# Down products of every second expert as seven block products

## The chip, the cores and the metric

The kernel runs on one NeuronCore of a Trainium2 chip. The time is the device time of one execution in microseconds, and the median of several executions is compared. All times of single stages come from one profiled execution.

## The reference

An attention layer over a small context is added to x, and then a mixture-of-experts layer, which is what matters here (cut, with T = 2048 tokens, D = 512, I = 256, 32 experts, 8 of them per token):

```python
comb = zeros((T, E)).at[rows, tidx].set(tw)      # weight of each token's 8 experts
g = einsum('td,eid->tei', x, w1)                 # up products
u = einsum('td,eid->tei', x, w3)
a = silu(g) * u
routed = einsum('tei,edi,te->td', a, w2, comb)   # down products, weighted
sh = silu(x @ shared_w1.T) * (x @ shared_w3.T) @ shared_w2.T
out = x + routed + sh
```

Everything is fp32.

## The kernel before

**Stages.** Attention, the gate and the routing come first (to about 183 us of the profiled span), with the shared expert's products as filler. From about 211 us the 32 experts are worked through, one place k after the other. The experts are ordered by how many tokens they have, and each place has a fixed width (`CAPS`, `ORDER`) and a fixed room for tokens (`ROOM`); `begins[k]` is where place k begins in a row of 138 slices of 128 token places. A slice can be shared by two neighbouring experts.

**Tokens.** `gather` (L1451) fetches the normalized rows of one slice from DRAM into a ring `xgs` of `NG_BUF` = 8 buffers, on GpSimd's queue. `transpose` (L1492) turns them in 32x32 blocks on VectorE, an instruction of L1501 picks the slice's weights into `wt`, and copies (L1489, nearly all on ScalarE) put the blocks in place as `x_of[k % 3]`.

**Up products.** For all experts but the first and the last, `seven(k)` does both up products as a 2x2 block product with seven block products (Strassen). `weight_sums` (L1556) and `token_sums` (L1585) form its operands on VectorE, `product` (L1594) is the matmul, and `add` (L1604), a bank copy (L1647), Silu (L1629) and a multiply (L1632) put the results together in `acts_of[k % 3]`. With h half of the room, an expert with more than 512 token places of room goes in two passes of seven steps, each step two matmuls of h columns; the others go in one pass of seven steps of four matmuls. The PSUM banks come from `ps_p`, a pool of six.

**Down products.** `down(j)` (L1735) does one slice j: two matmuls (the two halves of I, one after the other into the same bank) of 512 columns, or more, narrower ones where a slice is shared. Its bank comes from `ps_y` or `ps_z` in turn, one bank each. `evict` (L1751) scales by the token's weight on ScalarE into a buffer `yw` (4 of them), and `send` (L1707) adds the rows to the output in DRAM by an indirect DMA on GpSimd's queue; an expert's scatters follow those of the place before. After the last slice of an expert, `load_weights` brings the down weights of the expert three places on, on SyncE's queue.

**The order.** It is written out by hand: each engine works through its list in the order in which the program emits it. The main loop goes over pieces (two per expert) and their steps. In a step the next up product is emitted, then what is due from earlier steps (`soon(f, after)` puts a function on the list of a later step, `tick` emits them), then some of the VectorE and ScalarE side work, and then the down products planned for this step. An expert's down products so stand among the up products of the next:

```python
many = max(len(ready_downs) - KEPT, 0)
many = many if odd else -(-many // 2)
planned = [(2 * i + 1) * steps // (2 * many) for i in range(many)]
dues = [1.0 + 1.5 * planned.count(step) for step in range(steps)]
```

`sup` and `sdn` hold the shared expert's weights and are not used once its products are done, apart from a branch `rest()` that is taken only when an expert has more tokens than its room.

Of the kernel before, what the change touches and what calls it, by code (L numbers as in the profile page):

```python
# [9 lines left out]
F32 = mybir.dt.float32  # L10
F16 = mybir.dt.float16
I32 = mybir.dt.int32
AF = mybir.ActivationFunctionType
ALU = mybir.AluOpType
# [4 lines left out]
P = 128  # L19
# [8 lines left out]
NW = 3  # L28
# [18 lines left out]
def tile_xattn_moe(  # L47
# [22 lines left out]
    TB = 512  # L70
# [862 lines left out]
    def rest():  # L933


        with ExitStack() as ctx:
            keep = ctx.enter_context(tc.tile_pool(name="keep", bufs=1))
            for b in range(B):
                xs[b] = keep.tile([P, D], F32, name=f"xr{b}")
            wp = ctx.enter_context(tc.tile_pool(name="wp", bufs=2))  # L940
            comb = keep.tile([P, NT, E], F32, name="comb")
            nc.sync.dma_start(comb, rows.rearrange("(t p) d -> p t d", p=P)[:, :, D:])

            full = [P, NT, E]
            past = keep.tile(full, F32, name="past")
            nc.vector.tensor_tensor(
                past, logits, limit.unsqueeze(1).to_broadcast(full), ALU.is_ge
            )
            nc.vector.scalar_tensor_tensor(
                past, logits, float(-BIG // 2), past, ALU.is_lt, ALU.mult  # L950
            )
            nc.vector.tensor_tensor(comb, comb, past, ALU.mult)
            with tc.tile_pool(name="ps_tr", bufs=2, space=PSUM) as ps_tr:
                for b in range(B):
                    nc.sync.dma_start(xs[b], out[b])
                    xn2[b] = xnp.tile([P, D], F32, tag="xn2", name="xn2", bufs=4)
                    nc.sync.dma_start(xn2[b], rows[ts(b, P), 0:D])
                    gate_turn(b, ps_tr.tile([P, ND, P], F32, tag="tr", name="tr"))

            def expert_sum(up, dn, e=None):  # L960

                for k in range(NTB):
                    a = wp.tile([P, NI, TB], F32, tag="a", name="a")
                    for i in range(NI):
                        gu = [ps_gu.tile([P, TB], F32, tag="gu", name="gu") for _ in range(2)]
                        for w in range(2):
                            for d in range(ND):
                                nc.tensor.matmul(
                                    gu[w],
                                    lhsT=up[:, w, d, ts(i, P)],  # L970
                                    rhs=xnT[k][:, d, :],
                                    start=(d == 0),
                                    stop=(d == ND - 1),
                                )
                        sl = wp.tile([P, TB], F32, tag="sl", name="sl")
                        nc.scalar.activation(sl, gu[0], AF.Silu)
                        nc.vector.tensor_tensor(a[:, i, :], sl, gu[1], ALU.mult)
                    for b in range(4 * k, 4 * k + 4):
                        y = ps_y.tile([P, D], F32, tag="y", name="y")
                        for i in range(NI):  # L980
                            nc.tensor.matmul(
                                y,
                                lhsT=a[:, i, ts(b % 4, P)],
                                rhs=dn[:, i, :],
                                start=(i == 0),
                                stop=(i == NI - 1),
                            )
                        if e is None:
                            nc.vector.tensor_tensor(xs[b], y, xs[b], ALU.add)
                        else:  # L990
                            nc.vector.scalar_tensor_tensor(
                                xs[b], y, comb[:, b, e : e + 1], xs[b], ALU.mult, ALU.add
                            )

            flag = nc.values_load(
                not_small[0:1, 0:1],
                min_val=0,
                max_val=1,
                skip_runtime_bounds_check_because="a flag",
            )  # L1000
            with tc.If(flag > 0):
                attention_general()
                all_weights(comb)
                with ExitStack() as ph:
                    ps_gu = ph.enter_context(tc.tile_pool(name="ps_gu", bufs=4, space=PSUM))
                    ps_y = ph.enter_context(tc.tile_pool(name="ps_y", bufs=2, space=PSUM))
                    expert_sum(sup, sdn)
            with ExitStack() as ph:
                ps_gu = ph.enter_context(tc.tile_pool(name="ps_gu", bufs=4, space=PSUM))
                ps_y = ph.enter_context(tc.tile_pool(name="ps_y", bufs=2, space=PSUM))  # L1010
                for e in range(E):
                    up = wp.tile([P, 2, ND, I], F32, tag="up", name="up")
                    dn = wp.tile([P, NI, D], F32, tag="dn", name="dn")
                    for dst, of in ((up[:, 0], w1), (up[:, 1], w3), (dn, w2)):
                        nc.sync.dma_start(dst, of[e])
                    expert_sum(up, dn, e)
            for b in range(B):
                nc.sync.dma_start(out[b], xs[b])
# [35 lines left out]
    def experts(ups, in_order, later, products):  # L1054
# [7 lines left out]
        wup = [wp.tile([P, 2, ND, I], F32, name=f"wup{r}") for r in range(NW)]  # L1062
        wdn = [wp.tile([P, NI, D], F32, name=f"wdn{r}") for r in range(NW)]

        NG_BUF = 8
        xgs = wp.tile([P, NG_BUF, D + E], F32, name="xgs")
        for r in range(NG_BUF):
            nc.gpsimd.memset(xgs[:, r, :], 0.0)
# [444 lines left out]
        def soon(f, after=1):  # L1513
            jobs.setdefault(now + after, []).append(f)
# [232 lines left out]
            soon(lambda: evict(j, y))  # L1747

        def evict(j, y):
            yws[j] = late.tile([P, D], F32, tag="yw", name="yw", bufs=4)  # L1750
            nc.scalar.activation(yws[j], y, AF.Copy, scale=wt[:, j : j + 1])  # L1751
            for args in waiting:
                send(*args)
            waiting.clear()
            rows_of = {k: (a, b) for k, a, b, _ in experts_at(j)}
            ks = sorted(rows_of)
            send(j, ks[0], *rows_of[ks[0]])
            waiting.extend((j, k, *rows_of[k]) for k in ks[1:])

        n_turned = n_gathered = n_down = 0  # L1760

        def gather_next():
            nonlocal n_gathered
# [36 lines left out]
        x_only.close()  # L1800
        late = ctx.enter_context(tc.tile_pool(name="late", bufs=2, side="right"))
        KEPT = 2

        def fast(k):
            return 0 < k < E - 1

        def direct(n):
            banks = {}
# [11 lines left out]
        for n in range(len(pieces)):  # L1820
# [30 lines left out]
            if not odd and k:  # L1851
                lag = 3 if fast(k - 1) else 0
                whole = begins[k] // P
                new_downs = [(j, now + lag) for j in range(n_down, whole)]
                n_down = whole
            if k == E - 1 and odd:
                whole = pieces[n][1] // P
                new_downs = [(j, now) for j in range(n_down, whole)]
                n_down = whole
            ready_downs += new_downs  # L1860
            many = max(len(ready_downs) - KEPT, 0)
            many = many if odd else -(-many // 2)
            planned = [(2 * i + 1) * steps // (2 * many) for i in range(many)]
            dues = [1.0 + 1.5 * planned.count(step) for step in range(steps)]
            done = 0.0
            sides = [(side, sum(c for c, _ in side)) for side in (on_DVE, on_ACT)]
            lefts = [total for _, total in sides]
            for step in range(steps):
                next(of_k)
                tick()  # L1870
                done += dues[step]
                for i, (side, total) in enumerate(sides):
                    due = done / sum(dues)
                    while side and lefts[i] > total * (1 - due) + 0.01:
                        c, f = side.pop(0)
                        f()
                        lefts[i] -= c
                if k == E - 1:
                    planned += [step] * 2
                for _ in range(planned.count(step)):  # L1880
                    if n == last_piece and len(ready_downs) == 1:
                        break
                    if ready_downs and ready_downs[0][1] <= now:
                        down(ready_downs.pop(0)[0])
                    elif step + 1 < steps:
                        planned.append(step + 1)
                gather_next()
                now += 1
            assert not on_DVE and not on_ACT
            if odd:  # L1890
                assert next(of_k, None) is None
                if k + NW < E:
                    load_weights(k + NW, True, False)
        ready_downs += [(j, 0) for j in range(n_down, NS)]
        while jobs or ready_downs:
            tick()
            if ready_downs and ready_downs[0][1] <= now:
                down(ready_downs.pop(0)[0])
            now += 1
        for args in waiting:  # L1900
            send(*args)
# [71 lines left out]
```

## Time and profile before

| | us |
|---|---|
| median of three executions | 877.54 |
| lowest, highest | 875.84, 1122.57 |
| profiled execution, its own time | 876.15 |
| its span | 874.0 |
| TensorE busy | 861.2 |
| VectorE busy | 577.2 |
| ScalarE busy | 630.1 |
| GpSimd busy | 479.6 |

The span is the time from the first to the last instruction of the profiled execution; 2.15 us of its own time lie around it. A busy time is the union of an engine's instructions. Matmuls overlap in the records, [...] so that the distance between starts is what one costs. The granted TensorE clock was 0.996 of full speed.

### The profile page before, as it was taken

To read this page: it belongs to the slowest core of one execution; us is meant where nothing else is said; L and a number is where in the kernel's file an instruction comes from. 1 tells how busy PE (TensorE), PEld (TensorE's weight loads), DVE (VectorE), ACT (ScalarE), POOL (GpSimd) and SP (SyncE) were. 2 spreads that over 40 slices of the span, in tenths; PEclk is the share of its full clock that TensorE was granted. 3 is DMA by queue.
4 is the path that set the end of the run, shared out by engine and by line. 5 is a ranking of instruction groups with operands and counts; after the bars stand their busy time and mean duration, and the time that the engine had idled before them with its cause. 6 is when DMAs were issued, how large, how long until landed. Compare 5 with 4: busy or idle time off the path is not lost.

```text
span 874.0 us, 12974 instructions
## 1 busy us (share of the span) xinstructions
PE 861.2 (99%) x4015; PEld 539.8 (62%) x4015; DVE 577.2 (66%) x1424; ACT 630.1 (72%) x1117; POOL 479.6 (55%) x590
## 2 busy tenths in 40 slices
PE   9999999999999999999999999999999999999995
PEld 5344444545665666666666667676667777777763
DVE  7877778859866766666666667676666676676310
ACT  5889732538987786778877878777777877988621
POOL 4487560044545666565656566655566666543454
PEclk9999999999999999999999999999999999999998
DMA  9111112656667778787778787878688888875544
GB/s 307 60 49 44 56 50 73 214 153 206 194 153 166 183 187 206 157 180 179 167 182 188 177 197 188 192 192 177 168 184 181 202 183 186 186 174 114 90 77 53
DMA packets 59870, 137.10 MB, mean 157 GB/s; under 512 B 12168, under 2 KB 16392, under 8 KB 59792
## 3 DMA queue, kind: packets, MB, share of 16 engines
q0 software_dynamic: 32032, 69.25, 42.5%
q1 hardware_dynamic: 27680, 66.81, 22.3%
q8 instruction: 34, 0.56, 0.3%
q14 instruction: 44, 0.36, 0.1%
q10 hardware_dynamic: 80, 0.13, 0.0%
HBM read 96.71 MB, written 46.73 MB: 164 GB/s over the span
## 4 chain that ended last, share of the span: by engine, by line
PE 92%; POOL 3%; issue 2%; DMA 1%; ACT 0%; DVE 0%; POOLq 0%; ACTq 0%
PE p L1594 44%; PE y L1735 25%; PE gu L284 6%; PE sc L491 5%; PE oT L507 4%; PE y L1388 3%; PE x L461 2%; POOL out_dram L1707 2%; PE gu L1524 2%; DMA out_dram<-yw,token 1%; PE tok L1040 1%; PE lgT L568 0%; PE lg L583 0%; ACT p L501 0%; PE rank L1279 0%
## 5 line engine op out<-in xcount | busy, mean ns | idle before, releaser
L1489 ACT COPY xall<-blocks 32x512 f32<-32x512 f32 (+4 forms) x684 | 360.3, 527 | 10.8 <-DVE blocks L1492 0.9
L1707 POOL DMA_INDIRECT out_dram<-yw,token x150 | 244.8, 1632 | 221.4 <-ACT yw L1751 86.3
L1735 PE MATMUL y<-wdn,sa 128*128 128x512 f32 (+2 forms) x672 | 259.2, 594 | 0.0
L1451 POOL DMA_INDIRECT xgs<-rows,token x138 | 155.4, 1126 | 116.0 <-DVE token L1052 53.2
L1594 PE MATMUL p<-xall,wup 128*128 128x270 f32 (+27 forms) x720 | 185.4, 393 | 0.0
L1751 ACT ACTIVATE yw<-y,wt 128x512 f32<-128x512 f32 x138 | 94.7, 686 | 124.2 <-PE y L1735 65.2
L1594 PEld LDWEIGHTS p<-xall,wup 128*128 128x128 f32 x720 | 136.6, 190 | 44.2 <-issue 16.1
L1735 PEld LDWEIGHTS y<-wdn,sa 128*128 128x128 f32 (+2 forms) x672 | 100.9, 171 | 83.7 <-issue 72.2
L1594 PE MATMUL p<-t,s 128*128 128x270 f32 (+27 forms) x480 | 125.6, 394 | 0.0
L1604 DVE TENSOR_TENSOR z<-u,p 128x270 f32<-128x270 f32 (+27 forms) x96 | 48.8, 508 | 103.1 <-PE p L1594 102.9
L1594 PEld LDWEIGHTS p<-t,s 128*128 128x128 f32 x480 | 91.1, 190 | 37.6 <-issue 22.4
L1492 DVE STREAM_TRANSPOSE blocks<-xgs 128x512 f32<-128x512 f32 x138 | 97.2, 704 | 0.0
L501 ACT ACTIVATE p<-sc 128x1024 f32<-128x1024 f32 x64 | 62.1, 1023 | 13.6 <-PE sc L491 13.6
L1594 PE MATMUL p<-t,wup 128*128 128x270 f32 (+27 forms) x240 | 63.7, 396 | 0.0
L1594 PE MATMUL p<-xall,s 128*128 128x270 f32 (+27 forms) x240 | 63.4, 394 | 0.0
L1604 DVE TENSOR_TENSOR u<-u,p 128x270 f32<-128x270 f32 (+27 forms) x48 | 24.4, 509 | 57.6 <-PE p L1594 57.6
L1594 PEld LDWEIGHTS p<-t,wup 128*128 128x128 f32 x240 | 45.1, 190 | 24.8 <-issue 16.5
L284 PE MATMUL gu<-xall,sup 128*128 128x512 f32 x128 | 59.2, 602 | 0.0
L1594 PEld LDWEIGHTS p<-xall,s 128*128 128x128 f32 x240 | 45.3, 190 | 15.7 <-issue 6.3
L491 PE MATMUL sc<-qT,kz 32*128 32x512 f32 x256 | 44.2, 639 | 0.5 <-ACT p L501 0.2
L1585 DVE TENSOR_TENSOR t<-xall,t 128x540 f32<-128x540 f32 (+27 forms) x60 | 43.4, 724 | 1.0
L284 PEld LDWEIGHTS gu<-xall,sup 128*128 128x128 f32 x128 | 22.9, 190 | 23.1 <-issue 22.7
(218 smaller groups left out, 899.3 us busy)
## 6 DMA issues: line engine op xcount, KB each, us to landing
wup<-in_w_dram SPq DMA_DIRECT2D x64, 512.0 KB, 4.8
wdn<-in_w_dram SPq DMA_DIRECT2D x32, 512.0 KB, 6.1
rows<-xn SPq DMA_DIRECT2D x16, 256.0 KB, 2.0
out_dram<-x SPq DMA_DIRECT2D x16, 256.0 KB, 3.4
x<-in_x_dram SPq DMA_DIRECT2D x15, 256.0 KB, 5.9
out_dram<-yw,token POOLq DMA_INDIRECT x150, 5.2
xgs<-rows,token POOLq DMA_INDIRECT x138, 4.6
cTs<-in_cT_dram SPq DMA_DIRECT2D x4, 256.0 KB, 5.1
```

The lines of the kernel that those rows point to most:

```text
L284: nc.tensor.matmul(acc, lhsT=sup[:, w, d, ts(i, P)], rhs=xnT[k][:, d, :], start=(d == 0), stop=(d == ND - 1),)
L491: nc.tensor.matmul(scs[j // 2][:, j % 2], lhsT=kzs[b // 4 % 2][rows, b % 4, i, :], rhs=qT[rows], start=True, stop=True, tile_position=(j * ...
L501: nc.scalar.activation(p, sc, AF.Exp, scale=1.0 / HD**0.5)
L1451: nc.gpsimd.indirect_dma_start(out=t, out_offset=None, in_=rows[:, :], in_offset=bass.IndirectOffsetOnAxis(ap=token[:, j : j + 1], axis=0) ...
L1489: yield on_ACT, 1 + many, lambda dst=dst, of=of, copy=copy: copy(dst, of)
L1492: nc.vector.transpose(blocks[:, j % NB_BUF, :], xgs[:, j % NG_BUF, 0:D])
L1585: yield lambda o=out_, a=a, b=b: nc.vector.tensor_tensor(o, a, b, ALU.subtract)
L1594: nc.tensor.matmul(acc[:, i, 0:h], lhsT=w[:, i, d, :], rhs=x[:, d, :], start=(first and i == d == 0), stop=(i == outs[-1] and d == 1), ski ...
L1604: soon(lambda: nc.vector.tensor_tensor(out_, a, b, ALU.add))
L1707: ins = nc.gpsimd.indirect_dma_start(out=flat, out_offset=bass.IndirectOffsetOnAxis(ap=token2[:, k - 1 : k] if a else token[0:b, j : j + 1 ...
L1735: nc.tensor.matmul(y[c0:c1, :], lhsT=acts_of[k % NA][:, i, col : col + c1 - c0], rhs=wdn[k % NW][:, i, :], start=(i == 0), stop=(i == NI - 1),
L1751: nc.scalar.activation(yws[j], y, AF.Copy, scale=wt[:, j : j + 1])
```

## The change

The down products of an odd place k that has four whole slices from its first aligned one are done together. The four slices (512 tokens) by I = 256 and I = 256 by D = 512 are taken as 2x2 blocks, of 256 tokens, 128 of I and 256 of D; seven block products replace eight. `seven_downs(k)` is a generator of seven units. Each unit emits one block product, two matmuls of 256 columns, into one PSUM bank; the sums of operands and of results go to VectorE, one bank copy and the scalings to ScalarE. The operand sums are kept in `sup`, two intermediate results in `sdn`, and one operand sum is written over a block of the activations. The finished rows stand in tiles `yp` and are sent by the same four scatters. The banks come from `ps_p`, the six that the up products use.

The units stand in the list of down products with half the weight of a slice, and the plan counts weights instead of slices. The gather ring has six buffers instead of eight, `yw` three instead of four, and the branch that is not normally taken loads `sup` and `sdn` again.

```diff
-        NG_BUF = 8
+        NG_BUF = 6
...
-            yws[j] = late.tile([P, D], F32, tag="yw", name="yw", bufs=4)
+            yws[j] = late.tile([P, D], F32, tag="yw", name="yw", bufs=3)
...
+        def four_of(k):
+
+            if k % 2 == 0 or not fast(k):
+                return None
+            j = -(-begins[k] // P)
+            return j if (j + 4) * P <= begins[k + 1] else None
...
+            t1, t2, t3, t4, s1, s2, s4 = (sums_at[:, i] for i in range(7))
+            s3 = a21
+            p1, u2 = temps_at[:, 0], temps_at[:, 1]
...
+            def sum_of(to, a, b, op, after=1):
+                then(lambda: nc.vector.tensor_tensor(to, a, b, op), after)
...
+            def times(acc, a, b, first=True):
+                for r in range(2):
+                    nc.tensor.matmul(
+                        acc[:, r, :],
+                        lhsT=a[:, ts(r, P)],
+                        rhs=b,
+                        start=(first and r == 0),
+                        stop=(r == 1),
+                        skip_group_check=not first,
+                    )
...
+            pa = bank()
+            times(pa, a11, b11)
+            then(lambda: nc.scalar.copy(p1, pa))
+            for to, a, b in ((t1, b12, b11), (t2, b22, t1)):
+                sum_of(to, a, b, ALU.subtract)
+            for to, a, b, op in ((s1, a21, a22, ALU.add), (s2, s1, a11, ALU.subtract)):
+                sum_of(to, a, b, op)
+            yield
+            rows1, rows2 = (late.tile([P, 2, D], F32, tag="yp", name="yp") for _ in range(2))
+            settle()
+            times(pa, a12, b21, first=False)
+            scaled(rows1[:, :, 0:DH], pa, first, 1)
+            for to, a, b in ((t3, b22, b12), (s3, a11, a21), (s4, a12, s2), (t4, b21, t2)):
+                sum_of(to, a, b, ALU.subtract)
+            yield
+            pb = bank()
+            times(pb, s2, t2)
+            sum_of(u2, p1, pb, ALU.add)
+            yield
+            pc = bank()
+            times(pc, s1, t1)
+            sum_of(rows2[:, :, DH:], u2, pc, ALU.add)
+            yield
+            pd = bank()
+            settle()
+            times(pd, s3, t3)
+            sum_of(rows2[:, :, DH:], rows2[:, :, DH:], pd, ALU.add)
+            yield
+            times(pc, s4, b22, first=False)
+            sum_of(rows1[:, :, DH:], u2, pc, ALU.add)
+            scaled(rows1[:, :, DH:], rows1[:, :, DH:], first, 2)
+            sent_out(rows1, first, 2)
+            yield
+            settle()
+            times(pd, a22, t4, first=False)
+            sum_of(rows2[:, :, 0:DH], u2, pd, ALU.add)
+            scaled(rows2, rows2, second, 2)
+            sent_out(rows2, second, 3)
+            if (j + 4) * P == begins[k + 1] and k + NW < E:
+                load_weights(k + NW, False, True)
+            yield
...
+                if len(ks) == 1 and four_of(ks[0]) == j:
+                    steps = seven_downs(ks[0])
+                    of += [(lambda steps=steps: next(steps), ready, 1)] * 7
+                    j += 4
+                else:
+                    of.append((lambda j=j: down(j), ready, 2))
+                    j += 1
...
-            many = max(len(ready_downs) - KEPT, 0)
-            many = many if odd else -(-many // 2)
-            planned = [(2 * i + 1) * steps // (2 * many) for i in range(many)]
-            dues = [1.0 + 1.5 * planned.count(step) for step in range(steps)]
+            weights_of = [w for *_, w in ready_downs]
+            work = max(sum(weights_of) - 2 * KEPT, 0)
+            work = work if odd else -(-work // 2)
+            many = next(m for m in range(len(weights_of) + 1) if sum(weights_of[:m]) >= work)
```

## The prediction

> **What bounds the kernel now.** I read the busy table and the slices first, then the chain that ended last, then the list of waits, and last the time-ordered rows of single stretches. From the page (engines with share of the span, then 40 slices in tenths):
>
> ```profile
> PE 861.2 (99%) x4015; PEld 539.8 (62%) x4015; DVE 577.2 (66%) x1424; ACT 630.1 (72%) x1117; POOL 479.6 (55%) x590
> ...
> PE   9999999999999999999999999999999999999995
> ...
> PE 92%; POOL 3%; issue 2%; DMA 1%; ACT 0%; DVE 0%; POOLq 0%; ACTq 0%
> PE p L1594 44%; PE y L1735 25%; PE gu L284 6%; PE sc L491 5%; PE oT L507 4%; PE y L1388 3%; PE x L461 2%; POOL out_dram L1707 2%; PE gu L1524 2%; DMA out_dram<-yw,token 1%; PE tok L1040 1%; PE lgT L568 0%; PE lg L583 0%; ACT p L501 0%; PE rank L1279 0%
> ```
>
> TensorE is never idle until the last slice and carries 92% of the chain; the products that the change touches (y, L1735) are a quarter of it. Busy is not proof for a pipelined engine, so I look at who waits for whom (engine and line that waited, releaser: total us, times, longest us):
>
> ```profile
> DVE z L1604 <- PE p L1594: 108.4, 77, 2.8
> ...
> ACT yw L1751 <- PE y L1735: 65.2, 65, 3.1
> ...
> PEld p L1594 <- DVE own L1501: 1.9, 8, 0.2
> ```
>
> VectorE and ScalarE wait for TensorE. The longest line in which TensorE's expert products (L1594) wait for VectorE comes near the end of the answer, with 0.2 us at most. So a microsecond of matmul is worth a microsecond, as long as the other engines keep up.
>
> **The matmuls: what goes and what comes.** A group is taken only if an odd expert k from 1 to 29 has four whole slices of 128 aligned to its start. With the widths and places written in the kernel that holds for k = 1, 3, ... 25: 13 groups, 52 of 138 slices; 27 and 29 fail. TensorE's list grows by 78 matmuls, which is 13 x (14 - 8). Rows of the chain in order of time (start, us, line, records; an fp32 matmul leaves two records):
>
> ```profile
> 489.79 1.72 PE y L1735 x4
> ...
> 654.80 3.43 PE p L1594 x16
> ```
>
> A slice (two matmuls of 512 columns) takes 1.72 us, 0.430 a record. The second row is expert 20, whose halves are 256 columns: 0.214 a record. A group goes from 16 x 0.430 = 6.88 us to 28 x 0.214 = 6.00 us: 0.88 us less, over 13 groups **11 us less**. That is the ceiling, 1.3% of the time.
>
> Here a rule speaks against the change. The Trainium skill, "TensorE: Matmul & The Clock Gate", section "Back-to-back issue gap", says that in a stream of weight-load and matmul pairs both set the spacing, so that fewer columns don't buy proportionate time: 81 ns at 128 columns, 131 at 512. Interpolated, 256 columns would cost 97/131 = 0.74 of 512, an estimate from that page. Then a group's 28 records take 28 x 0.74 x 0.430 = 8.9 us, 2.0 more than now, and the whole 876 + 26 = 902 us. The row above is the same operand type at the same width with one weight load per record, and its ratio is 0.50. I take the row.
>
> **VectorE: what comes.** Per group eight 128x256 sums (the operands of the seven products) and five 128x512 adds out of PSUM; its list grows by 169 = 13 x 13 instructions. What counts is the distance between starts of neighbours. VectorE's rows in order of time (start, us, line, operation):
>
> ```profile
> 450.14 0.69 DVE L1556 TENSOR_TENSOR s<-wup,s 128x512 f32<-128x512 f32 x1
> 450.74 0.43 DVE L1604 TENSOR_TENSOR z<-z,p 128x270 f32<-128x270 f32 x1
> 451.09 0.70 DVE L1492 STREAM_TRANSPOSE blocks<-xgs 128x512 f32<-128x512 f32 x1
> ...
> 455.50 0.78 DVE L1585 TENSOR_TENSOR t<-xall 128x600 f32<-128x600 f32 x1
> 456.31 0.78 DVE L1585 TENSOR_TENSOR t<-xall,t 128x600 f32<-128x600 f32 x1
> ```
>
> A 512-wide sum lasts 0.69 but the next starts after 0.60; a 270-wide one 0.43 against 0.35. Only one that needs its neighbour's result (last two rows) waits out the whole duration and 0.03 more. So a slot is the duration less 0.08: 0.34 for 256 wide, 0.60 for 512. Per group 8 x 0.34 + 5 x 0.60, and 0.24 for two dependent pairs (t2 after t1, s2 after s1) = **6.0 us**. On the mean there is room (window, PE, PEld, DVE, ACT and POOL busy, clock, DMA):
>
> ```profile
> 381.90:423.90 42.00, 42.00 (x148) 27.83 (x147) 28.09 (x70) 33.77 (x65) 21.12 (x17) 1.00 0.73 168
> ```
>
> That is one pair of experts with one group: (28.1 + 6.0)/41.1 = 83%. But the group is dealt out over part of the pair. I laid VectorE's list against TensorE's for the group of expert 9, from the second unit (in the second pass of expert 10, h = 302) to the seventh (first pass of expert 11, h = 270). TensorE: 5 up products x 1.01 + 7 x 0.91 + the group's 6.0 = 17.5 us. VectorE, in slots: seven adds and multiplies at 0.39, two token sums at 0.63, four transposes with their owner sums at 0.76, a 604-wide multiply 0.79, four weight sums 2.5, five adds at 0.35: 12.1 us, and the group's 6.0: 18.1 us. **VectorE has 104% of the stretch to do**, where before it had 12.1 us in some 18. It cannot idle there, and falls about 0.7 us behind. An up product's sum is needed three products later, 3 us and more, which hides most of it.
>
> **ScalarE: what comes.** Four evictions (4 x 0.686, L1751) go. One copy of a whole bank (0.59, as qT, L482), four half-row scalings (0.38 each, as the 128x256 Silu, L1533) and two 512-wide ones out of SBUF (0.73, as kz, L375) come: 3.57 for 2.74, 0.8 us more per group, against 33.8 of 42 busy. But the bank copy is now waited for: the second unit accumulates into the bank that p1 is copied from, two up products (2.0 us) after the first, and the copy queues behind xall copies of up to 0.72 us each. Two of these ahead of it use the cover up.
>
> **The new waits, priced.** Behind TensorE's waiting instruction stands everything, since it works in order: a wait is lost time at once. A unit's banks now come out of the six that the up products rotate through, so up products also wait for the group's adds. Bounds: no wait at all (0 us); or VectorE at its full recorded durations with no overlap (21.1 us in a stretch of 17.5), which after the slack costs some 1.7 us a group, 21 in all. The rows show the overlap everywhere, so I go near the lower end. Laying the three lists side by side for all groups with the slots above, 0.2 us from a product to its reader (a record lasts 0.16 beyond the start of the next) and 0.25 us for TensorE to load weights again after a wait (0.19 a load), leaves eight waits of up to 1.0 us at second units for ScalarE (3.9 us) and seven for VectorE (1.8 us): **5.7 us**, 0.43 a group. With slots longer by 0.03 us it is 11, so this is the soft number.
>
> **Edits that cost nothing.** The gather ring goes from eight to six. The tightest place is at the start: slice 16's gather must now follow slice 10's owner sum (a gather starts at 216.88 right after it), 1.0 to issue and 4.6 to land give 222.5; its transpose starts at 224.71. Later a buffer has six slices of 4.9 us. Were this cover gone, each late gather would hold all of VectorE behind it. With three yw buffers, an eviction follows a scatter three slices back (some 15 us) against 1.6 to issue and 5.2 to land. Scatters keep their number, two bunched after each half group; GpSimd is busy 21 of 42 us. A down weight's load is issued after the seventh unit; SP's next loads follow it, and the tile is needed two experts (40 us) later against 6.1 to land. The reloads of sup and sdn stand in a branch not taken here. The end of the kernel (experts 27 to 31, the last scatters) is unchanged.
>
> **The sum.** Span 874.0, own time 876.15; - 11.0 + 5.7 = 870.8. The median shown is 877.54 and the lowest 875.84, so the profiled execution is within 0.2% of either. I say **871 us**. A measurement of this kernel can tell about 2% from no change, and no outcome in sight reaches that.
>
> **Rivals.** (1) *All of it arrives.* The waits are hidden by the three-product slack: 865. For it: VectorE idles a third of the time. Against it: the 104%. (2) *VectorE becomes the bound*, the other side: in the ten groups dealt out over two-pass experts its list is over-full, and each late sum stops TensorE. It decides from 0.85 us a group on; at full durations 876 - 11 + 21 = 886. The Trainium skill takes this side: "VectorE: DVE Perf Modes", section on the TRN2 errata, gives an fp32 sum (N + 151)/0.96 ns, 0.42 us for 256, and warns of small tiles, since each pays the fixed part. By it the 13 instructions cost 6.8 us instead of 5.7; the starts above say that 0.08 of each is overlapped. (3) *Both cancel*: slots longer by 0.03 cost 11 us, 876. (4) *Weight loads bound the narrow products*: 902. (5) *It doesn't do what it says*, groups falling back to single slices: the lists show all 13 made.
>
> **Chances.** Forecast (868 to 874) 0.45; all arrives (under 868) 0.15; cancelled (874 to 879) 0.18; VectorE bound (879 to 893) 0.15; beyond, by (4) or late gathers, 0.05; faster by more than the ceiling 0.02. Range: 865 to 885. By 2% (858.6 and 893.7): faster 0.02, same 0.92, slower 0.06.
>
> **What would show it.** Right: L1735 loses 208 records (52 slices of four), the new unit line shows 28 records per group at 0.214 to 0.216; TensorE's waits on the p1 copy and on adds sum to 3 to 9 us; VectorE's busy time grows by some 80 us. Wrong: records above 0.22 (rival 4), no waits of TensorE at all (rival 1), more than 11 us of them (rival 2), or waits for gathers in VectorE's list.

## The result and the profile after

The changed kernel takes **920.6 us** (median of six executions, 918.48 to 925.83) against 876.1 before (median of six; one of them, 1122.57, stands far above the other five, 875.84 to 877.54): a ratio of 1.051, interval 1.048 to 1.055. It is 5% slower. I had forecast 871 us, with a range up to 885 and a chance of 0.06 for slower.

The page of the profiled execution (span 921.6 us, 1.8 us more as its own time): busy per engine, TensorE and its granted clock in 40 slices, and the group of the single slices that are left.

```profile
PE 866.4 (94%) x4171; PEld 577.2 (63%) x4171; DVE 653.8 (71%) x1593; ACT 640.9 (70%) x1156; POOL 472.7 (51%) x588
...
PE   9999999999999999999896959699797999999995
...
PEclk9999999999999999999997979889898999999998
...
L1737 PE MATMUL y<-wdn,sa 128*128 128x512 f32 (+2 forms) x464 | 161.4, 595 | 0.0
```

TensorE was 99% busy and is 94% now. The 9s of its row drop in six slices between the 20th and the 31st (23 us each, so from 438 to 714 us), and the granted clock drops in the same stretch. All 13 groups are made: the single slices have 464 records, 208 fewer than before.

Next the list of waits of the changed kernel (engine and line that waited, releaser: total us, times, longest us):

```profile
ACT yw L1753 <- DMA out_dram<-yw,token: 62.4, 12, 6.8
...
PE y L1819 <- ACT sdn L1848: 41.8, 6, 9.7
POOL out_dram L1709 <- ACT xall L1491: 38.7, 15, 7.3
...
POOL out_dram L1709 <- DMA out_dram<-yp,token: 20.9, 4, 7.8
```

The second line is the loss: six waits of TensorE at a group's unit, for the copy of p1 on ScalarE, up to 9.7 us long. That is the wait that I had priced at up to 1.0 us. The first line is new as well: ScalarE's evictions wait 62 us for scatters to land. Before, no eviction waited for a DMA. To see how the two hang together I read one place on three engines, in order of time.

GpSimd in the changed kernel (start us, us, operation, and in brackets the idle time before it with its releaser); `yp` are a group's rows, `yw` a single slice's:

```profile
461.36 1.55 POOL L1709 DMA_INDIRECT out_dram<-yp,token  x1 [0.30 <-ACT yw L1753]
...
465.08 1.55 POOL L1709 DMA_INDIRECT out_dram<-yp,token  x1 [0.30 <-issue]
473.19 1.55 POOL L1709 DMA_INDIRECT out_dram<-yw,token  x1 [6.55 <-ACT xall L1491]
475.05 1.08 POOL L1453 DMA_INDIRECT xgs<-rows,token  x1 [0.30 <-issue]
476.43 1.04 POOL L1453 DMA_INDIRECT xgs<-rows,token  x1 [0.31 <-issue]
477.78 1.00 POOL L1453 DMA_INDIRECT xgs<-rows,token  x1 [0.30 <-issue]
479.09 1.62 POOL L1709 DMA_INDIRECT out_dram<-yw,token  x1 [0.30 <-issue]
```

The group's scatters leave one behind the other; then the queue stands for 6.55 us. The scatter of 473.19 is the first of the next place, and "an expert's scatters follow those of the place before". It goes 8.1 us after the last group scatter was issued, right behind that one's landing: the trace has the last of its landing events at 472.44, and the end of the queue's wait for them at 472.47. The releaser printed, an xall copy, is only the last semaphore by the profile. Behind it three gathers stand ahead of the next scatter of rows.

ScalarE in the same place (the same columns; one L1753 is one eviction):

```profile
460.61 0.69 ACT L1753 ACTIVATE yw<-y,wt 128x512 f32<-128x512 f32 x1
...
465.62 0.69 ACT L1753 ACTIVATE yw<-y,wt 128x512 f32<-128x512 f32 x1 [1.17 <-PE y L1737]
...
470.26 0.69 ACT L1753 ACTIVATE yw<-y,wt 128x512 f32<-128x512 f32 x1 [1.05 <-PE y L1737]
...
478.06 0.69 ACT L1753 ACTIVATE yw<-y,wt 128x512 f32<-128x512 f32 x1 [5.00 <-PE y L1737]
...
487.10 0.69 ACT L1753 ACTIVATE yw<-y,wt 128x512 f32<-128x512 f32 x1 [6.57 <-DMA out_dram<-yw,token]
...
491.42 0.59 ACT L1848 COPY sdn<-y 128x512 f32<-128x512 f32 x1
```

The rows evicted at 460.61 are scattered at 473.19, so the buffer is free at about 478, where the fourth eviction begins. The rows of 465.62 are scattered at 479.09 and land at 487.10, 21.5 us after their eviction, and there the fifth eviction begins. The wait of 5.00 is put down to a matmul that had ended by 474; it is the landing, whose last event stands at 477.86. ScalarE works in order, so the bank copy (last row) stands behind these evictions.

TensorE in the same place (x4 are the four records of a unit or an up product):

```profile
480.90 1.03 PE L1819 MATMUL y<-wdn,sa 128*128 128x256 f32 x4
481.76 1.17 PE L1596 MATMUL p<-t,s 128*128 128x300 f32 x4
482.77 1.17 PE L1596 MATMUL p<-xall,wup 128*128 128x300 f32 x4
492.06 2.07 PE L1819 MATMUL y<-wdn,sa 128*128 128x256 f32 x4 [8.11 <-ACT sdn L1848]
493.92 2.20 PE L1596 MATMUL p<-xall,wup 128*128 128x300 f32 x4
495.92 2.20 PE L1596 MATMUL p<-xall,s 128*128 128x300 f32 x4
497.92 1.08 PE L1819 MATMUL y<-sup 128*128 128x256 f32 x4
498.85 1.17 PE L1596 MATMUL p<-t,wup 128*128 128x300 f32 x4
```

The first unit takes 0.86 us to the next start, as forecast. Two up products later the second unit waits 8.11 us for the copy. What follows the wait runs at half the rate: the same unit takes 1.86, the up products 2.00 instead of 1.01. Full rate is back at 498.85. From 492.06 that is 6.79 us for work that takes 2 x 0.86 + 2 x 1.01 = 3.74: another 3.05 us lost.

Worked out in this way, the six waits are 2.74, 8.11, 9.68, 7.77, 7.91 and 5.57 us, 41.8 together, and the slow stretches behind them lose 1.64, 3.05, 3.04, 2.44, 2.23 and 1.89, 14.3 together. The sum is **56 us**. The span of the version without these waits (below) is 921.6 - 866.9 = 54.7 us shorter. So the loss is accounted for; the experiments have to say which edit makes it.

### The profile page after: what moved, and what is told of

Same layout as the page of the kernel before. It is cut to its first block, busy times and chain, and to the rows that moved or that the text cites. A ratio compares the mean times of both kernels' runs of the same rounds, so it can differ in the third digit from the quotient of the medians.

```text
span 921.6 us, 13511 instructions
## 1 busy us (share of the span) xinstructions
PE 866.4 (94%) x4171; PEld 577.2 (63%) x4171; DVE 653.8 (71%) x1593; ACT 640.9 (70%) x1156; POOL 472.7 (51%) x588
## 5 line engine op out<-in xcount | busy, mean ns | idle before, releaser
L1453 POOL DMA_INDIRECT xgs<-rows,token x138 | 150.3, 1089 | 216.5 <-DVE own L1503 133.1
L1709 POOL DMA_INDIRECT out_dram<-yw,token x98 | 156.4, 1596 | 131.2 <-ACT xall L1491 37.1
L1596 PE MATMUL p<-xall,wup 128*128 128x270 f32 (+27 forms) x720 | 190.4, 401 | 0.0
L1596 PEld LDWEIGHTS p<-xall,wup 128*128 128x128 f32 x720 | 139.5, 194 | 39.7 <-issue 11.9
L1737 PE MATMUL y<-wdn,sa 128*128 128x512 f32 (+2 forms) x464 | 161.4, 595 | 0.0
L1753 ACT ACTIVATE yw<-y,wt 128x512 f32<-128x512 f32 x86 | 59.0, 686 | 124.9 <-DMA out_dram<-yw,token 62.4
L1709 POOL DMA_INDIRECT out_dram<-yp,token x52 | 87.3, 1680 | 44.2 <-ACT yp L1831 16.1
L1737 PEld LDWEIGHTS y<-wdn,sa 128*128 128x128 f32 (+2 forms) x464 | 61.4, 162 | 54.7 <-issue 48.6
L1819 PE MATMUL y<-wdn,sa 128*128 128x256 f32 x104 | 33.2, 449 | 41.8 <-ACT sdn L1848 41.8
L501 ACT ACTIVATE p<-sc 128x1024 f32<-128x1024 f32 x64 | 62.1, 1024 | 13.5 <-PE sc L491 13.5
L1606 DVE TENSOR_TENSOR u<-p,p 128x270 f32<-128x270 f32 (+27 forms) x48 | 24.3, 507 | 40.1 <-ACT p L1649 33.0
L1819 PEld LDWEIGHTS y<-wdn,sa 128*128 128x128 f32 x104 | 22.0, 221 | 48.8 <-ACT sdn L1848 45.4
```

Source lines behind the costliest of these rows:

```text
L501: nc.scalar.activation(p, sc, AF.Exp, scale=1.0 / HD**0.5)
L1453: nc.gpsimd.indirect_dma_start(out=t, out_offset=None, in_=rows[:, :], in_offset=bass.IndirectOffsetOnAxis(ap=token[:, j : j + 1], axis=0) ...
L1596: nc.tensor.matmul(acc[:, i, 0:h], lhsT=w[:, i, d, :], rhs=x[:, d, :], start=(first and i == d == 0), stop=(i == outs[-1] and d == 1), ski ...
L1606: soon(lambda: nc.vector.tensor_tensor(out_, a, b, ALU.add))
L1709: ins = nc.gpsimd.indirect_dma_start(out=flat, out_offset=bass.IndirectOffsetOnAxis(ap=token2[:, k - 1 : k] if a else token[0:b, j : j + 1 ...
L1737: nc.tensor.matmul(y[c0:c1, :], lhsT=acts_of[k % NA][:, i, col : col + c1 - c0], rhs=wdn[k % NW][:, i, :], start=(i == 0), stop=(i == NI - 1),
```

## The experiments

### Which edit: the row buffers

The changed kernel gets its fourth yw buffer back, in the tile that holds the routing's logits. The logits are saved to DRAM and loaded again in the branch not taken.

```diff
-            yws[j] = late.tile([P, D], F32, tag="yw", name="yw", bufs=3)
+            if len(evicted) % 4 == 3:
+                yws[j] = logits.rearrange("p t e -> p (t e)")
+            else:
+                yws[j] = late.tile([P, D], F32, tag="yw", name="yw", bufs=3)
+            evicted.append(j)
```

> The changed kernel with a fourth yw buffer (its memory is the logits tile, saved to DRAM first). Theory A, the ring of three yw buffers: an eviction waits for a scatter three slices back, ScalarE stands behind it with the p1 copy, TensorE behind that; a fourth buffer takes most of the 42 us of TensorE waits away, 870 to 885 us. Theory B, the gather ring of six: gathers that wait for VectorE's owner sums stand in GpSimd's queue ahead of the scatters and delay them; a fourth yw buffer then only shortens the waits, 890 to 910. Theory C, VectorE has too much to do: no difference, 915 to 925.

Measured: **868.4 us** (867.30 to 868.87), ratio 0.991, interval 0.989 to 0.992. It is 52 us faster than the changed kernel, more than theory A expected, and the seven block products now win 0.9% over before. Its page (engines, and TensorE's 40 slices):

```profile
PE 851.9 (98%) x4171; PEld 570.1 (66%) x4171; DVE 650.5 (75%) x1593; ACT 640.6 (74%) x1156; POOL 475.4 (55%) x588
...
PE   9999999999999999999999999999999999999995
```

From its list of waits:

```profile
ACT yw L1762 <- DMA out_dram<-yw,token: 8.3, 2, 6.6
...
ACT logits L1762 <- DMA out_dram<-logits,token: 3.6, 3, 1.7
...
PE y L1828 <- DVE yp L1819: 1.0, 2, 0.5
...
PEld y L1828 <- ACT sdn L1857: 0.9, 3, 0.6
```

TensorE's waits for the bank copy are gone but for 0.9 us before weight loads, and the evictions (those into the fourth buffer, `logits`, included) wait 11.9 us for DMAs instead of 62.4. TensorE loses 14.5 us of busy time at the same 4171 instructions, as much as the slow stretches were worked out to cost.

Is it then the three buffers as such? The kernel before with each ring made smaller, and with both:

```diff
-            yws[j] = late.tile([P, D], F32, tag="yw", name="yw", bufs=4)
+            yws[j] = late.tile([P, D], F32, tag="yw", name="yw", bufs=3)
```

```diff
-        NG_BUF = 8
+        NG_BUF = 6
```

> The kernel before with three yw buffers instead of four, nothing else changed. Theory A in its strong form (three buffers are too few whatever the down products are): slower, 885 to 910 us. Theory A with the groups' bunched scatters as a needed part: within 3 us of 876. Theories B and C: 876.

> The kernel before with a gather ring of six instead of eight, nothing else changed. Theory B in its strong form: slower, 885 to 910 us. Theories A and C: 876, since gathers have some 28 us to spare. The rings only together would leave both this and the kernel with three yw buffers at 876.

> The kernel before with three yw buffers and a gather ring of six together. If the loss needs the groups: 876 us. If the two smaller rings do it only together: slower, 890 and more.

Measured: 875.97, 875.98 and 875.95 us; ratios 1.000, 1.000 and 1.000, all intervals within 0.9986 to 1.0008. Neither edit costs anything by itself, and they cost nothing together. The list of waits of the kernel before with three yw buffers shows how near it comes:

```profile
POOL out_dram L1707 <- DMA out_dram<-yw,token: 69.1, 18, 6.8
...
ACT yw L1751 <- DMA out_dram<-yw,token: 7.1, 4, 1.9
```

GpSimd waits for landings there too, 18 times and for up to 6.8 us, but ScalarE's evictions wait only four times, at most 1.9 us, and nothing follows from it. The loss needs the three buffers **and** the groups. What the groups change is seen at the same place in this kernel; GpSimd first,

```profile
456.02 1.83 POOL L1707 DMA_INDIRECT out_dram<-yw,token  x1 [0.30 <-issue]
464.69 1.58 POOL L1707 DMA_INDIRECT out_dram<-yw,token  x1 [6.83 <-DMA out_dram<-yw,token]
```

then ScalarE:

```profile
454.37 0.69 ACT L1751 ACTIVATE yw<-y,wt 128x512 f32<-128x512 f32 x1 [0.39 <-ACT xall L1489]
458.77 0.69 ACT L1751 ACTIVATE yw<-y,wt 128x512 f32<-128x512 f32 x1 [0.80 <-PE y L1735]
```

The wait between two places is as long as in the changed kernel (6.83 us against 6.55). But the place's last scatter leaves at 456.02, 2.8 us **ahead** of the next place's first eviction (458.77), whose rows go 5.9 us after it. In the changed kernel the last of the bunch leaves at 465.08, 4.5 us **behind** that eviction (460.61), and its rows go 12.6 us after it. The wait hasn't grown; it begins 7 us later as the evictions count.

The gather ring in the changed order, one buffer less with yw at four:

```diff
-        NG_BUF = 6
+        NG_BUF = 5
```

> The changed kernel with four yw buffers and a gather ring of five instead of six. A gather follows the owner sum that frees its buffer in the program's order whatever the ring's size, so if the ring only sets how early rows are fetched, nothing changes: 868 us, within 2. If the smaller ring took part in the loss (theory B), one buffer less must cost something here: 875 us and more.

Measured: 870.7 us, from 867.47 to 875.73. The range overlaps with that of six buffers (867.30 to 868.87) and reaches far above it, so a loss from five is neither shown nor excluded. For six, the forecast's "costs nothing" was seen only in the order before.

### The rival: VectorE as the bound

My rival (2) also gives more than 11 us of waits at the units. The eight operand sums of each group are left out, first in the changed kernel and then with the fourth yw buffer:

```diff
-            for to, a, b in ((t1, b12, b11), (t2, b22, t1)):
-                sum_of(to, a, b, ALU.subtract)
...
+            t1 = b12
+            t2 = b22
+            s1 = a21
+            s2 = a22
```

> The changed kernel without the eight 128x256 operand sums of each group: the seven products take plain blocks, so the down products of the groups are not those of the reference. VectorE loses 2.9 us of work a group, 38 us in all. Theory C (VectorE over-full): most of the loss goes, 870 to 885 us. Theories A and B: the long waits of TensorE for the p1 copy stay, 905 to 922 us.

> Four yw buffers and no operand sums (plain blocks, so the groups' rows are not those of the reference). It prices what VectorE's eight sums a group still cost once the long waits are gone. From 868.4: the prediction's sum with no waits gives 865; if VectorE's sums cost nothing any more, 868.

Measured: **917.7 us** (ratio 1.048, interval 1.046 to 1.051) and 866.1 us (0.988, 0.986 to 0.989). The list of waits of the first:

```profile
ACT yw L1753 <- DMA out_dram<-yw,token: 50.8, 10, 7.3
...
PE y L1819 <- ACT sdn L1848: 38.8, 6, 9.4
```

With 104 instructions off VectorE's list the same two waits stand there. By the medians the sums are worth 2.9 us here, where the ranges overlap, and 2.3 us with four buffers, where they don't. This rival is refuted, most plainly by the version with four row buffers: VectorE has as much to do in it as in the changed kernel (650.5 us busy against 653.8). How full VectorE may be is seen in one window of the version with four yw buffers (stretch; then us, and busy us of TensorE, its weight loads, VectorE, ScalarE, GpSimd; clock, DMA share, GB/s):

```profile
475.00:495.00 20.00, 20.00 (x88) 16.53 (x87) 19.19 (x47) 17.84 (x42) 12.58 (x10) 1.00 0.86 235
```

VectorE is busy 19.2 of 20 us in it and TensorE doesn't stop.

### Why the buffers stay occupied

In the changed kernel (three yw buffers) the four scatters of each group are left out:

```diff
-                        yws[at] = rows[:, r, :]
-                        send_all(at)
+                        for args in waiting:
+                            send(*args)
+                        waiting.clear()
```

> The changed kernel (three yw buffers) without the four scatters of each group: their rows are missing from the output. Theory A1, the group's four scatters, issued together and awaited by the next place's first scatter, are what holds the yw buffers: the long waits of TensorE go, 862 to 872 us. If three buffers are too few next to the groups for another reason (gathers in the queue, late evictions): 895 to 920.

Measured: **864.4 us**, ratio 0.986, interval 0.984 to 0.988. Three buffers are enough when the group sends nothing. But this takes away two things at once: GpSimd's time for 52 scatters, and the next place's wait for their landing. To part them, the same scatters, as many and as large, go to a tensor of their own in DRAM, which no other scatter has to follow:

```diff
-                        yws[at] = rows[:, r, :]
-                        send_all(at)
...
+                        ins = nc.gpsimd.indirect_dma_start(
+                            out=to[:, :],
...
+                            in_=rows[:, r, :],
...
+                            compute_op=ALU.add,
```

> The changed kernel (three yw buffers) with the four scatters of each group sent to a DRAM tensor of their own, one per group, so that their rows are missing from the output. GpSimd issues as many scatters and as many bytes move, but the next place's first scatter no longer waits until these four have landed. Theory A1 in the narrow sense, that wait for landing holds the queue: 865 to 880 us. If the queue time of four bunched scatters (1.9 us each) is what delays the others: 895 to 920.

Measured: **870.0 us**, ratio 0.993, interval 0.991 to 0.994. GpSimd in the same place as above, in this kernel:

```profile
463.44 1.55 POOL L1849 DMA_INDIRECT aside<-yp,token  x1 [0.30 <-issue]
465.30 1.55 POOL L1709 DMA_INDIRECT out_dram<-yw,token  x1 [0.30 <-issue]
```

and from its list of waits:

```profile
ACT yw L1753 <- DMA out_dram<-yw,token: 21.6, 12, 3.5
...
PE y L1821 <- ACT sdn L1868: 2.6, 3, 1.7
```

The scatter that went at 473.19 goes at 465.30, straight behind the group's last. With the work of GpSimd and the DMA queues unchanged, 50.6 of the 52 to 56 us are gone. So the scatters' time on the queues is not the main cause: together with all else that the two versions differ in, it costs at most the 5.6 us to the version without them, and evictions still wait for landings 12 times, but for 3.5 us at most. The cause is the next place's wait for the bunch to land. Spreading the bunch out with that wait kept was not tried.

Last, the gathers that stand between two scatters of rows. They are emitted right after the step's due work instead of at its end. A gather whose buffer comes free by the side work of a step so leaves one step later, behind the scatters that are due there:

```diff
                 tick()
+                gather_next()
...
-                gather_next()
```

> The changed kernel (three yw buffers) with each gather emitted one step later, behind the scatters of that step and after the owner sum that it waits for. Theory A2, gathers that wait for owner sums stand ahead of scatters in GpSimd's queue and are what delays them: most of the loss goes, 870 to 890 us. Theory A1, the scatters wait for the landing of the place before: it stays at 905 to 922.

Measured: 898.1 us, ratio 1.026, interval 1.022 to 1.030: between the two ranges expected, so both theories were too simple. Its list of waits:

```profile
ACT yw L1753 <- DMA out_dram<-yw,token: 36.1, 10, 5.8
...
PE y L1819 <- ACT sdn L1848: 19.3, 5, 6.7
```

Half of TensorE's waits go (19.3 of 41.8 us stay), and 22.5 of the 52 us of loss. GpSimd's rows at the same place show what the edit changes:

```profile
469.35 1.56 POOL L1709 DMA_INDIRECT out_dram<-yw,token  x1 [6.37 <-DMA out_dram<-yp,token]
471.21 1.08 POOL L1453 DMA_INDIRECT xgs<-rows,token  x1 [0.30 <-issue]
472.60 1.58 POOL L1709 DMA_INDIRECT out_dram<-yw,token  x1 [0.31 <-issue]
```

The wait for the landing is as long as before (6.37 us), but one gather stands behind it instead of three, and the second scatter of rows goes 3.25 us after the first instead of 5.90. So the wait for the landing starts the delay; the gathers behind it, 1.4 us each from start to start, lengthen it for the second row buffer. Taking away the dependency itself was not tried: two scatters in flight could then add to the same row.

### A better version

The fourth buffer and the moved gathers together:

> Both remedies: four yw buffers, and each gather emitted a step later behind the scatters. If what waits are left with four buffers come from the queue: 865 to 867 us; if they come from VectorE's and ScalarE's work: 868, as with four buffers alone.

Measured: **866.9 us** (866.44 to 869.05), ratio 0.990, interval 0.988 to 0.992. This and the fourth buffer alone beat both kernels, the one before by about 1%; between the two no difference is shown. With four buffers GpSimd's queue still stands at the same place, as its rows in order of time in the version without the moved gathers show:

```profile
461.02 1.79 POOL L1712 DMA_INDIRECT out_dram<-yp,token  x1 [0.30 <-issue]
468.77 1.55 POOL L1712 DMA_INDIRECT out_dram<-logits,token  x1 [5.96 <-ACT xall L1494]
```

It waits 5.96 us for the landing, and that is hidden: the extra buffer is one more slice of time.

## Why the prediction was wrong

**The step that failed** stands under "Edits that cost nothing": "With three yw buffers, an eviction follows a scatter three slices back (some 15 us) against 1.6 to issue and 5.2 to land. Scatters keep their number, two bunched after each half group". The 15 us were about right: the evictions of 460.61 and 470.26, two slices apart, lie 9.7 us from each other. What I set against them was wrong. I took the scatter to leave as soon as its rows were there. Measured from eviction to free buffer it is 17.5 and 21.5 us: 12.6 and 13.5 from the eviction until the scatter goes, then 4.9 and 8.0 from the start of the issue to the eviction that its landing lets go, where I had 6.8. So the missing term is the time until the scatter goes. I had named the bunching (as two and two; here four leave in a row), and ahead of the prediction stood the sentence that a place's scatters follow those of the place before, but I never put the two together: the next place's first scatter must wait for the end of the bunch, and GpSimd's list is in order. The waits for landings were there to be read before the change, in the kernel's own list:

```profile
POOL out_dram L1707 <- DMA out_dram<-yw,token: 53.2, 12, 6.3
```

**The wait on the p1 copy** was found in the right place and given the wrong size. I counted what ScalarE does ahead of the copy (xall copies of 0.72 us), but not what ScalarE itself may wait for. A list in order passes on the waits of everything ahead of the instruction, here an eviction that waits for a DMA.

**The price of a stopped TensorE** was a second mis-sized term: 0.25 us to load weights again, where the six waits show 1.6 to 3.05 us on top, 14.3 in all. The trace's record of the granted clock has six stretches at half before TensorE's work ends, each beginning within one of the six waits. The one of the stall shown above, as a window (columns as before):

```profile
487.80:498.04 10.24, 5.98 (x13) 4.27 (x14) 7.25 (x20) 9.98 (x23) 2.53 (x2) 0.50 0.33 80
```

The granted clock is 0.50, and 5.98 of the 10.24 us are TensorE's work behind the wait. The Trainium skill, "TensorE: Matmul & The Clock Gate", Part 1, says that the clock falls to half after an idle window of some 3.4 us and comes back after about as much work. The half rate (2.00 for 1.01) agrees; the work until the full clock was back took 3.2 to 6.0 us behind the six waits, and a wait of 2.74 us, shorter than the page's window, was enough for it here.

**What held.** A unit costs 0.86 us, 0.215 a record, so narrow products cost in proportion, and rival (4) with the page's 902 us is refuted. The ceiling of 865 us is met by the kernel without the group's scatters, 864.4, though that one also has fewer scatters to issue. VectorE's busy time grew by 653.8 - 577.2 = 76.6 us, forecast 13 x 6.0 = 78. The 104% of a stretch did little harm. With the stalls gone, 868.4 less 876.1 - 11.0 = 865.1 leaves 3.3 us for all new waits, where I had 5.7; leaving the sums out takes 2.3 of them. My forecast of 871 describes the version with four row buffers to within 2.6 us, in part by luck: of the 3.9 us that I had put down for waits on the bank copy, 0.9 is there.

**What I listed as signs** was too coarse. "More than 11 us" of waits at the units was to mean rival (2); it came, 41.8 us, from something else. A sign should name the releaser's own wait, not only the amount. None of my five rivals contained a scatter.

**What stays open.** Only six of the 13 groups stall. GpSimd's list shows a pattern that no run tested. The five longest stalls, at k = 11 to 19, each follow a group (k = 9 to 17) whose four scatters leave in a row with the next place's first scatter right behind them. At k = 1 to 7 one or two more scatters of the same place come in between, and the groups after them don't stall, but for the one at k = 9 with the shortest wait, 2.74 us. At k = 19, 21 and 23 another slice's scatter stands between two pairs, and the groups after them don't stall either. At k = 19 these are that scatter and the first of the second pair:

```profile
722.72 1.58 POOL L1709 DMA_INDIRECT out_dram<-yw,token  x1 [2.87 <-ACT sg L1631]
728.85 1.55 POOL L1709 DMA_INDIRECT out_dram<-yp,token  x1 [4.54 <-DVE own L1503]
```

A plan that sends the bunch in two pairs may then do without the fourth buffer; this was not tried.

## What to carry to other kernels

Before a ring of buffers is made smaller, follow a buffer to the instruction that frees it, and ask what that instruction's own queue waits for, not only how long it lasts. When work is regrouped, look not only at how many transfers there are but at when they leave: a bunch ahead of an ordering wait delays everything behind it on that queue. TensorE, once stopped, paid twice here, for the wait and for the slow restart.

## What was not expected of the hardware

After waits of 2.7 to 9.7 us TensorE ran its next products at about half the rate, and each wait cost 1.6 to 3.05 us more than its own length. It doesn't show as idle time: the products at half rate count as busy, which is why TensorE was busy 866.4 us in the changed kernel and 851.9 with four row buffers, for the same instructions.
